# Macaron block on one core: routing found in two parts, the last expert rows loaded over one queue, and a list in a new order

## The chip, the core and the metric

The kernel runs on one core of a Trainium2 chip. The metric is device time in microseconds (us) for one execution. All times below are us unless marked otherwise. The engines are TensorE (PE, with its weight loads shown apart as PEld), VectorE (DVE), ScalarE (ACT), GpSimd (POOL) and SyncE (SP). SP, ACT and POOL can also issue DMAs.

## What is computed

The input is 8 sequences of 512 tokens of width 128, in fp32. Three layers follow each other, each on a normalised copy of the residual stream `x`:

```python
x = x + 0.5 * ffn(layernorm(x), ...)
x = x + attn(layernorm(x), ...)
x = x + 0.5 * ffn(layernorm(x), ...)
```

The same FFN weights serve both times. It is a mixture of experts:

```python
normed = layernorm(x) * ln_gamma + ln_beta
probs = softmax(normed @ router_w.T)            # 8 experts
top_v, top_i = top_k(probs, 2)
gates = softmax(top_v)
comb = sum(one_hot(top_i, 8) * gates[..., None])
out = sum over e of comb[:, e] * swiglu(normed, gate_up_w[e], down_w[e])   # inner width 384
out = out + swiglu(normed, shared_gate_up_w, shared_down_w)                # inner width 128
```

`swiglu` is `silu(gate) * up @ down`. The attention works in windows of 128 tokens and keeps the 32 largest of each row's 128 scores. It adds its own residual and a second normalisation.

## The kernel before, in words

**Blocks and groups.** The 4096 tokens are 8 blocks of 512 (4 windows of 128 each), in two groups: blocks 0 to 3 and 4 to 7. Each FFN runs once for each group. So there are four expert rounds, named (key, group): (0,0), (0,1), (1,0) and (1,1). Attention runs block by block between the rounds of the first FFN and those of the second: blocks 0 to 3 beside round (0,1), blocks 4 to 7 beside round (1,0).

**From logits to sorted rows.** `norm` (L532) normalises a block, writes its rows to DRAM (`rows`), transposes it, and makes the router's logits (`lg`, L563), which DVE copies into `lgs` (L568). `route` (L593) waits for all four blocks of a group. It makes the softmax (L607 to L614, with an exp on ACT at L611), takes the largest and the second largest of 8 (`first`, L620 to L629, twice, with L632 between), sums both choices (`own`, L647), and counts them over the tokens (`csum`, L648 to L653, and two matmuls, `rank`, L664). From these it gets each row's place among the rows sorted by expert. 32 small matmuls (`inv`, L731) invert that order into `src` (L742), the list of rows to gather.

**Expert rounds.** `experts` (L832) handles 39 tiles of 128 sorted rows. POOL gathers rows from DRAM (L846, 32 gathers for a round), PE transposes four of them at a time (`xTp`, L858), ACT applies scale and bias into `xT` (L863). For each tile, `pair` (L875) brings the weights of that tile's expert (`wt`: SP loads them from DRAM at L901, or DVE copies them from SBUF at L899 in the rounds of `COPIED`), then PE makes gate `pg` and up `pu` (L924), ACT the silu (L932), DVE the product (L935), PE the down product `y` (L940). ACT copies `y` to `yb` (L954), and POOL scatters it to `ys` in DRAM (`put`, L962, 39 scatters for a round).

**Back to the tokens.** `fetch_back` (L972) loads each token's two expert rows (`yg`, two loads of 256 KB for a block). `combine` (L990) multiplies them by the gates and adds them to `x` on DVE (L999, four steps for each of the two). For blocks 4 and 6 of the second FFN (`LAST_ON_PE`), `weigh` makes diagonal matrices of the gates, and `combine_on_pe` (L1021) sums on PE: for each window a product of the identity with `x` and two products of a diagonal with `yg`, 12 matmuls in one operation (L1030); ACT copies the sum back to `x` (L1035). `write` (L1137) stores the block. In the last group the first of a block's two loads is issued by SP (L987), the second by ACT (L984), and the blocks come in the order 4, 6, 5, 7.

**What sets the order.** Nothing is issued as it is written. Every operation is recorded with its engine, a cost, what it reads and writes, and a due time (`Plan.op`, L107). `Plan.schedule` (L144) then lets time run: each engine takes, of the operations that could start first, the one with the smallest due time; and a buffer's slot is given when its first user starts. The list that comes out is the program's order on every engine, and each engine works it off in that order. The due times come from constants by hand (`PACE`, `LAG`, `SHARED`, `ROUTE_B`, `FINISH` and so on, L62 to L69). Where this list leaves PE idle for over 0.75, `emit` (L235) puts in matmuls whose result nobody reads (`unread`, L448), so many that they fill the gap but for 0.4. PSUM is planned as seven banks: at most four for `pg` and `pu`, one for `y`, three for everything else (`ps_m`), seven in all.

Of the kernel before, what the change touches and what calls it, by code (L numbers as in the profile page):

```python
# [19 lines left out]
W = 4  # L20
# [25 lines left out]
LAST = 4  # L46
LAST_ON_PE = (4, 6)
# [14 lines left out]
PACE = (1.79, 2.74, 2.54, 0.71)  # L62
LAG, STRETCH, ROUTE_STRETCH = 10.7, -1.72, 3.22
NORM_B, NORM_LAG, NORM_STRETCH = 7.11, 0.69, 1.39
SHARED = ((58.99, 4.72), (33.75, 29.05))
SHARED1 = ((79.31, 10.55), (5.29, 29.83))
ROUTE_B = 39.98
PAIRS, PUTS = 0.2, 10.21
FINISH = 21.26  # L69
# [183 lines left out]
def kernel(  # L253
# [338 lines left out]

    def route(key, g):  # L593
# [6 lines left out]
        def t(tag, shape, dtype=F32):  # L600
            return buf(shape, tag, f"{tag}_{key}_{g}", dtype)

        lgs, alls = r.lgs, [(r.lgs, i) for i in range(GB)]
        mx, sm, m0, m1, i0, th = (t(n, [P, GW, 1]) for n in ("mx", "sm", "m0", "m1", "i0", "th"))
        pr, eq, o0, o1, own = (t(n, full) for n in ("pr", "eq", "o0", "o1", "own"))
        B = 0.29
        dve(B, lambda: ve.tensor_reduce(mx()[:, :, 0], lgs(), AX.X, ALU.max), alls, [mx],  # L607
            after=[(before_[3], 0.0)])
        dve(B, lambda: ve.tensor_tensor(pr(), lgs(), mx().to_broadcast(full), ALU.subtract),
            [*alls, mx], [pr])  # L610
        act(0.29, lambda: nc.scalar.activation(pr(), pr(), AF.Exp), [pr], [pr], table="exp")  # L611
        dve(B, lambda: ve.tensor_reduce(sm()[:, :, 0], pr(), AX.X, ALU.add), [pr], [sm])
        dve(0.25, lambda: ve.reciprocal(sm(), sm()), [sm], [sm])
        dve(B, lambda: ve.tensor_tensor(pr(), pr(), sm().to_broadcast(full), ALU.mult),  # L614
            [pr, sm], [pr])

        dve(B, lambda: ve.scalar_tensor_tensor(pr(), pr(), TINY, pr(), ALU.is_ge, ALU.mult),
            [pr], [pr])

        def first(o, m):  # L620

            dve(B, lambda: ve.tensor_reduce(m()[:, :, 0], pr(), AX.X, ALU.max), [pr], [m])
            dve(B, lambda: ve.tensor_tensor(eq(), pr(), m().to_broadcast(full), ALU.is_equal),
                [pr, m], [eq])
            dve(B, lambda: ve.tensor_tensor(eq(), eq(), rev8.to_broadcast(full), ALU.mult),
                [eq], [eq])
            dve(B, lambda: ve.tensor_reduce(i0()[:, :, 0], eq(), AX.X, ALU.max), [eq], [i0])
            dve(B, lambda: ve.tensor_tensor(
                o(), rev8.to_broadcast(full), i0().to_broadcast(full), ALU.is_equal), [i0], [o])  # L629

        first(o0, m0)
        dve(B, lambda: ve.scalar_tensor_tensor(pr(), o0(), -4.0, pr(), ALU.mult, ALU.add),  # L632
            [o0, pr], [pr])
        first(o1, m1)

        gates = r.gates = t("gates", [P, 2, GW])
        floor, plan.floor = plan.floor, max(plan.floor, plan.ops[-1].due + 30.0)
        dve(0.17, lambda: ve.tensor_tensor(th(), m0(), m1(), ALU.subtract), [m0, m1], [th])
# [8 lines left out]
        dve(B, lambda: ve.tensor_tensor(own(), o0(), o1(), ALU.add), [o0, o1], [own])  # L647
        dve(0.23, lambda: ve.tensor_copy(csum[0][:, PAD:, :], own()), [own], ["cs0"])  # L648
# [18 lines left out]
        pe(0.7, count, [f"cs{i}", own], [rankb])  # L667
# [16 lines left out]
        for k, o in ((0, o0), (1, o1)):  # L684
            dve(B, lambda o=o: ve.tensor_tensor(eq(), o(), at(), ALU.mult), [o, at], [eq])
            dve(B, lambda k=k: ve.tensor_reduce(posf()[:, k, :], eq(), AX.X, ALU.add),
                [eq], [(posf, k)])
# [187 lines left out]
    def pair(r, key, g, t, pace, came, first, upto):  # L875
# [81 lines left out]
        for i in range(a, b):  # L957
            def put(t=c * CH + i, i=i):
                if last_put:
                    nc.gpsimd.memset(apart, 0.0)  # L960
                last_put.append(t)
                ins = nc.gpsimd.indirect_dma_start(  # L962
                    r.ys, bass.IndirectOffsetOnAxis(ap=r.dst()[:, t : t + 1], axis=0),
                    yb()[:, i, :], None,
                ).ins

                tc.declare_no_dep(ins, group=group, reason="rows of other tokens")
                tc.add_to_no_dep_group(group, ins)

            plan.op("POOL", 1.33, put, [(yb, i), r.dst], [(group, c * CH + i)], lat=3.4)  # L970

    def fetch_back(key, b):  # L972
# [9 lines left out]
        for k in range(2):  # L982
            if key and g == NG - 1 and k:
                plan.op("ACT", 0.6, lambda: nc.scalar.dma_start(yg[1](), ys_t[i, 1]),  # L984
                        written, [yg[1]], lat=4.0)
            else:
                load(0.6, yg[k], lambda k=k: ys_t[i, k], written, [yg[k]], lat=4.0)  # L987
        return yg

# [31 lines left out]
    def combine_on_pe(b, yg, diag):  # L1021
# [3 lines left out]
        def both():  # L1025
            for w in range(W):
                for j, (lhsT, rhs) in enumerate(
                    ((ident, xs[b]), (diag[0](), yg[0]()), (diag[1](), yg[1]()))
                ):
                    nc.tensor.matmul(  # L1030
                        sum_()[:, w, :], lhsT if j == 0 else lhsT[:, w, :], rhs[:, w, :],
                        start=j == 0, stop=j == 2)

        pe(2.65, both, [*diag, *yg, xk], [sum_])
# [106 lines left out]
    def blocks(g):  # L1141
        return range(g * GB, (g + 1) * GB)
# [24 lines left out]
    for g in range(NG):  # L1167
# [20 lines left out]
        for b in sorted(blocks(g), key=lambda b: b % 2):  # L1188
# [45 lines left out]
```

## Time and profile before

| | us |
|---|---|
| runs before | 528.71, 529.16, 531.62, 534.18 |
| median of them | 530.39 |
| the profiled execution's own time | 529.42 |
| its span | 527.7 |
| PE busy | 496.7 (94%) |
| PE weight loads busy | 462.7 (88%) |
| DVE busy | 381.3 (72%) |
| POOL busy | 369.8 (70%) |
| ACT busy | 276.8 (52%) |

The profiled execution is one run of the program; its own time holds 1.7 beside the span of the records. "Busy" is the time with an instruction in work, and for PE it includes the filler matmuls (L448: 280 half-passes; an fp32 matmul is two). An fp32 matmul of 128 columns shows as two records that start 0.112 apart. The largest groups are the expert matmuls `pg`, `pu` and `y` (936 records each) and POOL's 156 scatters and 128 gathers of about 1.0 each.

### The profile page before, as it was taken

What the parts mean: (1) busy time and instruction counts of PE and PEld (TensorE: products, weight loads), DVE (VectorE), ACT (ScalarE), POOL (GpSimd) and SP (SyncE); (2) the same over time, 40 slices, a digit from 0 to 9 for tenths busy, and PEclk for the clock granted to TensorE, in tenths of its full rate; (3) what the DMA queues carried; (4) which work ended last, traced back from release to release, by engine and by line L of the source; (5) the groups of instructions that cost most, each with busy time, mean ns of one, the idle gap of its engine ahead of it and who ended that gap; (6) DMA issues with size and microseconds to landing.
All of it is one profiled execution on the core that took longest, in us unless ns stands there. A gap on an engine that the chain in (4) does not pass through costs nothing.

```text
span 527.7 us, 13534 instructions
## 1 busy us (share of the span) xinstructions
PE 496.7 (94%) x4080; PEld 462.7 (88%) x4080; DVE 381.3 (72%) x1440; ACT 276.8 (52%) x588; POOL 369.8 (70%) x481
## 2 busy tenths in 40 slices
PE   3999999999999999999999989999999999999996
PEld 2977899989998989889888888889998999999995
DVE  6589887565349999985598999996479647744413
ACT  4924334333434999976522687997664333333310
POOL 7305888878877786888536886988836778878840
PEclk9979999999999999999999999999999999999998
DMA  7941111111378344556626443545666136311134
GB/s 225 331 166 34 54 46 52 51 51 51 116 261 310 105 147 147 173 147 192 180 95 207 157 137 103 157 133 185 188 200 193 61 96 208 93 46 51 52 119 157
DMA packets 39611, 72.27 MB, mean 137 GB/s; under 512 B 7604, under 2 KB 17848, under 8 KB 39544
## 3 DMA queue, kind: packets, MB, share of 16 engines
q1 hardware_dynamic: 29880, 51.73, 31.1%
q0 software_dynamic: 9088, 18.63, 11.1%
q10 hardware_dynamic: 576, 1.05, 0.5%
q8 instruction: 38, 0.62, 0.5%
q14 instruction: 29, 0.24, 0.1%
HBM read 54.86 MB, written 16.52 MB: 135 GB/s over the span
## 4 chain that ended last, share of the span: by engine, by line
PE 66%; DVE 15%; DMA 6%; POOL 5%; issue 4%; ACT 3%; POOLq 0%; ACTq 0%
PE pg L924 16%; PE y L940 15%; PE pu L924 15%; DVE tk L1088 3%; DVE am L1084 3%; PE ysh L588 2%; DMA wt<-in_expert_gu 2%; PE unread L448 2%; PE pgs L579 2%; DMA xg<-rows,src 2%; PE pus L582 2%; POOL xg L846 2%; PE xTp L858 2%; PE lg L563 2%; DVE sc L1103 2%
## 5 line engine op out<-in xcount | busy, mean ns | idle before, releaser
L962 POOL DMA_INDIRECT ys<-yb,dst x156 | 159.4, 1022 | 55.7 <-issue 25.6
L846 POOL DMA_INDIRECT xg<-rows,src x128 | 128.5, 1004 | 71.1 <-issue 40.1
L924 PE MATMUL pg<-xT,wt 128*128 (+1 forms) x936 | 132.0, 277 | 7.1 <-issue 3.4
L940 PE MATMUL y<-ew,s 128*128 x936 | 129.6, 277 | 2.4 <-DVE s L935 2.1
L924 PE MATMUL pu<-xT,wt 128*128 (+1 forms) x936 | 130.4, 275 | 0.1
L924 PEld LDWEIGHTS pg<-xT,wt 128*128 128x128 f32 x936 | 117.5, 192 | 14.3 <-issue 8.8
L932 ACT ACTIVATE s<-pg 128x384 f32<-128x384 f32 x156 | 75.9, 489 | 99.3 <-PE pg L924 97.2
L940 PEld LDWEIGHTS y<-ew,s 128*128 128x128 f32 x936 | 116.7, 192 | 9.1 <-DVE s L935 3.8
L924 PEld LDWEIGHTS pu<-xT,wt 128*128 128x128 f32 x936 | 117.0, 192 | 0.5 <-DVE s L935 0.3
L935 DVE TENSOR_TENSOR s<-pu,s 128x384 f32<-128x384 f32 x156 | 85.4, 550 | 39.0 <-PE pu L924 27.5
L899 DVE COPY wt<-egu 128x768 f32 x78 | 44.6, 571 | 54.9 <-PE pu L924 53.5
L954 ACT COPY yb<-y 128x512 f32<-128x512 f32 (+1 forms) x60 | 26.1, 436 | 38.4 <-PE y L940 37.8
L999 DVE SCALAR_TENSOR_TENSOR x<-yg,gates,x 128x128 f32<-128x128 f32 x112 | 35.7, 383 | 11.8 <-DMA yg<-ys 11.8
L448 PEld LDWEIGHTS unread<-ident 128*128 128x128 f32 x280 | 33.0, 193 | 2.8 <-issue 2.8
L863 ACT ACTIVATE xT<-xTp,gb 128x512 f32<-128x512 f32 (+2 forms) x34 | 25.3, 754 | 19.3 <-PE xTp L858 19.2
L448 PE MATMUL unread<-ident 128*128 128x128 f32 x280 | 33.9, 276 | 0.0
L499 ACT ACTIVATE n<-x,nb,rstd 128x128 f32<-128x128 f32 x56 | 22.8, 484 | 5.0 <-DVE nb L479 3.9
L1088 DVE MATCH_REPLACE8 tk<-am,tk 128x128 f32<-128x128 f32 x96 | 25.4, 275 | 0.0
L581 ACT ACTIVATE ss<-pgs 128x512 f32<-128x512 f32 x16 | 9.6, 598 | 25.2 <-PE pgs L579 25.2
L858 PE MATMUL xTp<-ident,xg 128*128 128x128 f32 x128 | 20.1, 274 | 2.3 <-DMA xg<-rows,src 2.3
L512 PE MATMUL nTp<-ident,n 128*128 128x128 f32 x64 | 13.1, 350 | 8.7 <-DVE n L489 8.3
L1084 DVE MAX8 am<-tk 128x8 f32<-128x128 f32 x96 | 20.7, 278 | 0.0
(177 smaller groups left out, 700.6 us busy)
## 6 DMA issues: line engine op xcount, KB each, us to landing
wt<-in_expert_gu SPq DMA_DIRECT2D x78, 384.0 KB
yg<-ys SPq DMA_DIRECT2D x28, 256.0 KB
rows<-n SPq DMA_DIRECT2D x16, 256.0 KB
egu<-in_expert_gu SPq DMA_DIRECT2D x8, 384.0 KB
ys<-yb,dst POOLq DMA_INDIRECT x156
x<-in_x SPq DMA_DIRECT2D x8, 256.0 KB
xg<-rows,src POOLq DMA_INDIRECT x128
out_x<-x SPq DMA_DIRECT2D x8, 256.0 KB
```

Of the source, the lines that this page charges most:

```text
L448: plan.idle = lambda: nc.tensor.matmul(unread, ident, ident, start=True, stop=True)
L846: nc.gpsimd.indirect_dma_start(xg()[:, j, :], None, r.rows, bass.IndirectOffsetOnAxis(ap=r.src()[:, t : t + 1], axis=0),)
L858: nc.tensor.transpose(tp()[:, w, :], xg()[:, w, :], ident)
L899: nc.vector.tensor_copy(to, egu[:, bass.ds(row, 2 * FF)])
L924: nc.tensor.matmul(p()[:, f, :], wt()[:, c * NF + f, :], xT[:, bass.ds(offs[1], P)], start=True, stop=True,)
L932: act(0.49, lambda: nc.scalar.activation(s(), pg()[:, 0:NF, :], AF.Silu), [pg], [s], table="silu")
L935: dve(0.56, lambda: nc.vector.tensor_tensor(s(), pu()[:, 0:NF, :], s(), ALU.mult), [pu, s], [s])
L940: nc.tensor.matmul(y()[:, j, :], s()[:, f, :], ew[:, bass.ds(offs[0] + f * H, H)], start=(f == 0), stop=(f == NF - 1),)
L962: ins = nc.gpsimd.indirect_dma_start(r.ys, bass.IndirectOffsetOnAxis(ap=r.dst()[:, t : t + 1], axis=0), yb()[:, i, :], None,).ins
L999: nc.vector.scalar_tensor_tensor(xs[b][:, w, :], yg[k]()[:, w, :], gates()[:, k, q : q + 1], xs[b][:, w, :], ALU.mult, ALU.add,)
L1084: ve.max(m8()[:, w, :], src()[:, w, :])
L1088: ve.match_replace(tk()[:, w, :], m8()[:, w, :], src()[:, w, :], TAKEN)
```

## The change

There are five edits.

1. `route` no longer takes the two experts of all 16 windows of a group in one chain of DVE steps. A new function, `best_two`, does the same steps for a slice of windows, and is called twice: for the first three blocks (`EARLY = 3`, 12 windows) and for the fourth (4 windows). The tiles are the same; the plan counts each tile's two parts apart. The exp on ACT is there twice as well. The gates, and all from `csum` on, stay in one part.
2. In the last group (round (1,1)) all eight loads of expert rows are issued by SP, in a fixed order, with costs of 0.5 and a latency of 2.8 in the plan; its scatters are planned with a latency of 2.4 instead of 3.4.
3. `combine_on_pe` records three operations instead of one: the identity with `x` as one 512-wide matmul, then the four products with the first rows, then the four with the second.
4. The blocks of a group are finished in the order 4, 5, 6, 7 (and 0, 1, 2, 3) instead of the even ones first.
5. The constants of the due times are new, so the whole list comes out in a new order on every engine.

```diff
+EARLY = 3
-PACE = (1.79, 2.74, 2.54, 0.71)
-LAG, STRETCH, ROUTE_STRETCH = 10.7, -1.72, 3.22
-NORM_B, NORM_LAG, NORM_STRETCH = 7.11, 0.69, 1.39
-SHARED = ((58.99, 4.72), (33.75, 29.05))
-SHARED1 = ((79.31, 10.55), (5.29, 29.83))
-ROUTE_B = 39.98
-PAIRS, PUTS = 0.2, 10.21
-FINISH = 21.26
+PACE = (2.51, 2.74, 2.41, 0.71)
+LAG, STRETCH, ROUTE_STRETCH = 13.21, -3.15, 3.38
+NORM_B, NORM_LAG, NORM_STRETCH = 4.21, -0.9, 1.2
+SHARED = ((54.98, 7.11), (47.75, 30.5))
+SHARED1 = ((55.52, 10.55), (7.41, 29.83))
+ROUTE_B = 33.63
+PAIRS, PUTS = 1.02, 20.88
+FINISH = 9.66
...
+    def best_two(r, lgs, part, at, came, mx, sm, m0, m1, i0, th, pr, eq, o0, o1, own):
+        ve, n = nc.vector, at.stop - at.start
+        full = [P, n, NE]
+        B = 0.13 + 0.01 * n
...
+        def do(fn, r, w, us=B, **k):
+            dve(us, fn, [(x, part) for x in r], [(x, part) for x in w], **k)
+
+        dve(B, lambda: ve.tensor_reduce(mx()[:, at, 0], one(lgs), AX.X, ALU.max),
+            came, [(mx, part)], after=[(before_[3], 0.0)])
+        dve(B, lambda: ve.tensor_tensor(one(pr), one(lgs), wide(mx), ALU.subtract),
+            [*came, (mx, part)], [(pr, part)])
+        act(0.29, lambda: nc.scalar.activation(one(pr), one(pr), AF.Exp),
+            [(pr, part)], [(pr, part)], table="exp")
+        do(lambda: ve.tensor_reduce(sm()[:, at, 0], one(pr), AX.X, ALU.add), [pr], [sm])
+        do(lambda: ve.reciprocal(one(sm), one(sm)), [sm], [sm], us=0.2)
+        do(lambda: ve.tensor_tensor(one(pr), one(pr), wide(sm), ALU.mult), [pr, sm], [pr])
+        do(lambda: ve.scalar_tensor_tensor(one(pr), one(pr), TINY, one(pr), ALU.is_ge, ALU.mult),
+           [pr], [pr])
+        rev = rev8[:, 0:1, :].to_broadcast(full)
+        for o, m in ((o0, m0), (o1, m1)):
+            if o is o1:
+                do(lambda: ve.scalar_tensor_tensor(
+                    one(pr), one(o0), -4.0, one(pr), ALU.mult, ALU.add), [o0, pr], [pr])
+            do(lambda m=m: ve.tensor_reduce(m()[:, at, 0], one(pr), AX.X, ALU.max), [pr], [m])
+            do(lambda m=m: ve.tensor_tensor(one(eq), one(pr), wide(m), ALU.is_equal),
+               [pr, m], [eq])
+            do(lambda: ve.tensor_tensor(one(eq), one(eq), rev, ALU.mult), [eq], [eq])
+            do(lambda: ve.tensor_reduce(i0()[:, at, 0], one(eq), AX.X, ALU.max), [eq], [i0])
+            do(lambda o=o: ve.tensor_tensor(one(o), rev, wide(i0), ALU.is_equal), [i0], [o])
+        do(lambda: ve.tensor_tensor(one(own), one(o0), one(o1), ALU.add), [o0, o1], [own])
...
+        B, parts = 0.29, ((0, EARLY), (EARLY, GB))
+        for part, (a, z) in enumerate(parts):
+            best_two(r, lgs, part, slice(a * W, z * W), [(lgs, i) for i in range(a, z)],
+                     mx, sm, m0, m1, i0, th, pr, eq, o0, o1, own)
...
-            plan.op("POOL", 1.33, put, [(yb, i), r.dst], [(group, c * CH + i)], lat=3.4)
+            plan.op("POOL", 1.33, put, [(yb, i), r.dst], [(group, c * CH + i)],
+                    lat=2.4 if (key, g) == (1, NG - 1) else 3.4)
...
-            if key and g == NG - 1 and k:
-                plan.op("ACT", 0.6, lambda: nc.scalar.dma_start(yg[1](), ys_t[i, 1]),
-                        written, [yg[1]], lat=4.0)
-            else:
-                load(0.6, yg[k], lambda k=k: ys_t[i, k], written, [yg[k]], lat=4.0)
+            last = key and g == NG - 1
+            after = [(order_[0], 0.0)] if last else ()
+            o = load(0.5 if last else 0.6, yg[k], lambda k=k: ys_t[i, k], written, [yg[k]],
+                     lat=2.8 if last else 4.0, after=after)
+            if last:
+                order_[0] = o
...
-        def both():
-            for w in range(W):
-                for j, (lhsT, rhs) in enumerate(
-                    ((ident, xs[b]), (diag[0](), yg[0]()), (diag[1](), yg[1]()))
-                ):
-                    nc.tensor.matmul(
-                        sum_()[:, w, :], lhsT if j == 0 else lhsT[:, w, :], rhs[:, w, :],
-                        start=j == 0, stop=j == 2)
-
-        pe(2.65, both, [*diag, *yg, xk], [sum_])
+        pe(0.85, lambda: nc.tensor.matmul(sum_(), ident, xs[b], start=True, stop=False),
+           [xk], [sum_])
+        for k in range(2):
+            def add(k=k):
+                for w in range(W):
+                    nc.tensor.matmul(
+                        sum_()[:, w, :], diag[k]()[:, w, :], yg[k]()[:, w, :],
+                        start=False, stop=k == 1 and w == W - 1)
+
+            pe(0.9, add, [diag[k], yg[k]], [sum_])
...
-        for b in sorted(blocks(g), key=lambda b: b % 2):
+        for b in blocks(g):
```

In the program that comes out, the filler matmuls are 107 instead of 140 (31 instead of 44 after the last `y`, 32 instead of 57 between the logits of block 3 and the first `pg` of round (1,0)). ACT has 30 loads of a function table instead of 24. DVE has 72 more rows of instructions. The identity products of blocks 4 and 6 (`sum_4`, `sum_6`) stand far ahead of the tail: the first among the tiles of round (1,0), the second ahead of the first transposes of round (1,1). The `yg` loads of blocks 4 to 7 for attention stand on SP behind the first three `wt` loads of round (1,0); before, those of blocks 4 and 5 stood ahead of them. All shared-expert work of the second FFN now stands ahead of round (1,1). From the first gather of round (1,1) on, POOL has 73 indirect DMAs instead of 76. On ACT the four DMA issues of the last group are gone; SP issues all eight in the order of the blocks.

## The prediction

> **What bounds the kernel now.** First the page: TensorE (PE) is busy 94% of the span.
>
> ```profile
> span 527.7 us, 13534 instructions
> ## 1 busy us (share of the span) xinstructions
> PE 496.7 (94%) x4080; PEld 462.7 (88%) x4080; DVE 381.3 (72%) x1440; ACT 276.8 (52%) x588; POOL 369.8 (70%) x481
> ```
>
> A busy PE is not all work: the list of groups has 280 half-passes of filler matmuls (`unread`, L448), 140 in the program's list. So I cut the span into seven stages at fixed points of PE's list (first `pg` of expert round (0,0); logits of block 3 in the second FFN; first `pg` of (1,0); logits of block 7; first `pg` of (1,1); last `y`; end) and asked for each stage's engine times. Columns: stretch, its length, PE, PEld, DVE, ACT and POOL busy (instructions), PE clock, DMA share, GB/s.
>
> ```profile
> 0.00:46.91 46.91, 37.24 (x214) 30.32 (x215) 34.41 (x170) 22.66 (x51) 17.09 (x41) 0.93 0.62 206
> 46.91:253.65 206.74, 201.38 (x1679) 188.79 (x1678) 154.34 (x566) 118.13 (x246) 164.73 (x199) 1.00 0.40 126
> 253.65:289.01 35.36, 32.66 (x283) 29.45 (x281) 28.58 (x117) 11.00 (x24) 18.27 (x27) 1.00 0.50 159
> 289.01:382.36 93.35, 88.94 (x723) 82.48 (x721) 81.37 (x366) 74.11 (x160) 77.16 (x84) 1.00 0.49 151
> 382.36:419.59 37.23, 36.19 (x312) 33.10 (x311) 29.40 (x99) 18.84 (x46) 20.75 (x32) 1.00 0.50 158
> 419.59:507.25 87.66, 84.92 (x745) 83.40 (x744) 48.80 (x110) 30.66 (x60) 70.33 (x100) 1.00 0.28 88
> 507.25:527.70 20.45, 15.35 (x138) 15.15 (x136) 4.38 (x16) 1.44 (x3) 1.47 (x3) 0.92 0.49 161
> ```
>
> Then I counted PE's real work in each stage, in the program lists of both kernels, at start-to-start times of this trace: 0.67 for three expert matmuls, 0.86 for a 512-wide matmul, 0.89 for eight 128-wide passes, 0.44 for four transposes. Work before/after, and fillers before/after: stage 1 20.2/20.3, 24/24; 2 195.4/193.6, 5/11; 3 19.0/22.2, 57/32; 4 84.4/90.4, 9/3; 5 35.1/31.3, 0/6; 6 83.3/81.5, 1/0; 7 5.4/3.6, 44/31. Both kernels hold 442.8 us of work; only idle time can go. It lies in stage 1, in stage 3 (35.36 long with 19.0 of work: the second FFN's first routing is exposed) and in stage 7.
>
> The chain of waits shows the two stalls that the change reaches:
>
> ```profile
> 283.85 3.40 DMA xg<-rows,src
> ...
> 435.20 5.50 DMA xg<-rows,src
> ...
> 507.41 9.83 PE unread L448 x88
> 517.24 5.38 PE sum L1030 x48
> ```
>
> In stage 3 the routing ends in `inv` (276.05 to 277.03); then the chain has 2.40 of sequencer time, POOL's gathers, and the fourth gather's landing, 3.40; fillers cover it. The line at 435.20 is the same gather with eight `yg` loads in flight on SP: 5.50. At the end PE does 9.83 of fillers and then the sums. The timeline of the tail (start, length, engine):
>
> ```profile
> 510.24 1.76 SPq L317 DMA_DIRECT2D yg<-ys  x4
> 510.24 1.81 ACTq L984 DMA_DIRECT2D yg<-ys  x4
> 516.83 1.14 DVE L999 SCALAR_TENSOR_TENSOR x<-yg,gates,x 128x128 f32<-128x128 f32 x4 [10.72 <-DMA yg<-ys]
> ...
> 519.08 3.24 DVE L999 SCALAR_TENSOR_TENSOR x<-yg,gates,x 128x128 f32<-128x128 f32 x12 [1.11 <-DMA yg<-ys]
> ```
>
> The trace's semaphore events put block 4's two loads at 513.6 and 513.8, but fillers held PE until 517.24. DVE started at 516.83, when block 5's first landed, and paused until block 7's at 519.06.
>
> **The change part by part.** Own time 529.42, span 527.7; the profiled run is 0.97 under the median 530.39 of the four runs, beside the two quick ones (528.71, 529.16). Sums are against 529.42.
>
> Tail (stage 7). Times from the last `y`'s end (507.42). The last put still lands so that SP issues 2.82 later (510.24). ACT loses four DMA issues (1.81), SP gets eight (3.66 in the row at 431.96, against 1.76). That earlier row is eight loads on one queue, beside POOL's traffic: they landed 2.64, 3.58, 4.87, 5.57, 6.24, 7.20, 7.89 and 8.70 after the first issue. With that: block 5's loads are third and fourth, at 7.7 and 8.4; four DVE steps are 1.14, so block 5 is done at 10.0; block 7's land at 10.7 and 11.5, done 13.0. Block 7's store then stands alone in the queue; block 4's took 2.35 from issue (520.57) to landing (522.92), so 15.4, and the program's end came 1.25 after the last landing: 16.7. Before: 527.71 - 507.42 = 20.3, so -3.6. PE: 31 fillers end at 6.8, block 4's sums at 8.6, block 6's wait for its landings (9.1, 10.0) and end at 10.9, their copy (0.59) at 11.7: not last. If the loads move without POOL at the tail's own 374 GB/s (0.7 each), it is -5.0; if a straggler lands as block 7's did here (9.0 after the issue), -3.0. I take -3.8, near the one-queue row.
>
> The identity step. Two 512-wide matmuls (0.86 each) go from the tail into stages 4 and 5, where PE is the bound: 1.72 is paid there, and counted in the work above. `sum_4` and `sum_6` then hold two of seven PSUM banks through stage 6; that leaves one for `y` and four for `pg`/`pu`, one less when a transpose needs it. No row shows this; the nearest is ACT's copy of a transpose, 0.79, which holds a bank. Bounds 0 to 12 (eight transposes of 1.5 each: 0.44, two handovers, 0.79); I take 0, since a `pg` bank is free again after its silu (0.49), long before its turn two pairs (4.0) later.
>
> Routing in two parts (stage 3). Before, the fourth block's copy is at 254.65, `own` ends at 265.92 and the gathers' source 278.66. A dependent DVE step of 128x128 starts every 0.32 (258.50, 258.82, 259.14); a 128x32 step is 0.19 in the copy's row, so some 0.20: 18 steps give 2.2. The list has the three blocks' last seven steps and two products between them, yet fewer waits for PE: adding its steps up I get 9.8 from the copy to the last `csum` against 13.3, 3.5 less. Middle: -2.9. One more product (0.55) stands in the later chain: +0.5. SP now sends three `wt` loads and then seven `yg` loads, where four `yg` loads went ahead of the routing's end before: the fourth gather lands beside them, 3.40 at best, 5.50 at worst; I take +0.4 of 2.1, as the `wt` loads were beside it already. Stage 3 is as long as this chain: -2.0. The list itself gives nearly that, 25 fillers fewer (-5.6) and 3.2 more work: -2.4. Bounds: -5.0 if no gap is left beside the fillers, 0 if a landing of 5.50 eats it. In stage 1 the four blocks' logits come together, so the split gains nothing; the third block's ACT work moves behind others, and exp runs twice: 0 to +0.8, +0.4.
>
> Exp twice. ACT loads a table for exp and one for silu at each routing:
>
> ```profile
> 255.92 1.28 ACT L611 ACT_TABLE_LOAD   x1
> 257.22 0.31 ACT L611 ACTIVATE pr<-pr 128x128 f32<-128x128 f32 x1
> ...
> 257.70 1.28 ACT L932 ACT_TABLE_LOAD   x1
> ```
>
> The program's list has 30 loads after and 24 before: 6 x 1.28 = 7.7 more of ACT, 2.9 at a time with the exp, in routings (0,1), (1,0) and (1,1). Behind it queue the silus, and PE for their banks: here PE stood 1.22 (258.73 to 259.95), at routing (1,1) 0.32. So 0.3 to 1.2 each, or nothing where PE has other work: +0.5 in stage 2, +0.3 in stage 5; in stage 3 PE waits for the chain anyway.
> The Trainium skill ("ScalarE: Activation LUTs", What ACT_TABLE_LOAD costs) speaks against this: a change of set is a load of about 1283 ns and a drain of about 1380, 2.66 in all. The load agrees, but the silu follows its load at 259.00 at once, so the trace shows no drain; by the page ACT's bill would be an estimated 16 instead of 7.7, and the sum, with three stalls longer by a drain, an estimated 529.3 instead of 525.2.
>
> The list anew. Stage 2: work -1.8, six fillers more at 0.223 = +1.3, tables +0.5: 0.0. Stage 4: work +6.0 (five pairs stand ahead of block 4's transposes, since its loads come late), six fillers fewer -1.3: +4.6, if the attention's gaps stay. Stage 5: work -3.8, fillers +1.3, tables +0.3: -2.2; less work now covers the last routing. Stage 6: work -1.8; the one gather wait of 1.03 goes, but the second chunk's gathers stand behind two puts, six issues of 1.3 and a landing after the first, some 1.6 late: -1.2. Each of stages 2 and 4 may be off by 2.5, stages 5 and 6 by 1.5: the gaps of a new order are not in this trace.
>
> Sum: +0.4 + 0.0 - 2.0 + 4.6 - 2.2 - 1.2 - 3.8 = -4.2, so 525.2.
>
> **The rivals.**
> All idle time that the shorter filler list stands for goes: stages 2 to 6 by work and fillers alone are -0.5 - 2.4 + 4.6 - 2.5 - 1.8 = -2.6, stage 3 gains up to 2.5 more, the tail reaches -5.0: 519.3 to 523; middle 521. For it: the tail's landings are in the trace. Against: in stage 3 idle time was 16.3 where fillers were 12.7, so a list promises more than it gives.
> POOL and the gathers take the gain: both landings go to 5.50 (+1.7 in stage 3, +2.1 in stage 5): 529.0. Also, from the first gather of (1,1) to the last put there are 73 indirect DMAs; before, 76 of them took 98.93 (409.06 to 507.99), 1.32 each, so 95.0 by POOL. PE needs 9.6 to the first `pg` (as 279.42 to 289.01), 81.5 of work, 3.4 of gaps and 0.6: 95.1. POOL is as late as PE, and a stall cannot be made up. With one of the two: 527 to 529. For it: POOL ran without pause there. Against: it had caught up by the end, where it waited for ACT before its last two puts (0.42 and 0.23).
> Slower: the two held PSUM banks. If every transpose of stage 6 waits, 8 x 1.5 = 12: 537.2. It decides from 0.53 for each of the eight, 4.2 in all. For it: no free bank is left. Against: the margin of 4.0 above.
> That the routing does not run early can be told from the lists: in stages 2 to 5 the three blocks' steps do stand ahead; in stage 1 they don't.
>
> **How the numbers follow.** Forecast 0.50 (522 to 528.5), all idle time gone 0.20, POOL and gathers 0.20, banks 0.10. A measurement of this kernel can tell about 1% from no change: 525.1 to 535.7 around 530.39. The forecast lies on that bound, so half of it counts as faster: 0.25 + 0.20 + 0.02 = 0.47; slower is most of the banks' case, 0.08; the rest, 0.45, is within 1%. Stage errors together (the root of the squares of 2.5, 2.5, 2.2, 1.5, 1.5 and 1) are about 4.8; 8 in 10 is 1.3 times that, 6.2: 519.0 to 531.4.
>
> **What would show it.** Tail right: DVE's first `yg` step within 8 of the last `y`, one unbroken filler run of about 6.9, the end 16 to 17.5 after the last `y`. Routing right: `inv` done with no filler ahead of it in stage 3, and a stage of 32 to 34. Wrong: gathers landing over 5 in stages 3 or 5; PE waiting for ACT's `xT` or silu in stage 6; a stage 4 of over 100, which would mean that the late start of block 4 is not made up.

## The result and the profile after

The changed kernel takes 529.73 (median of 52 runs, 526.26 to 534.32), the kernel before 531.13 (78 runs, 526.16 to 534.66); the ratio is 0.9984 with a 95% interval of 0.9972 to 0.9996. So the change gains 0.9 by the ratio (0.2 to 1.5); 525.2 was forecast, 4.2 less than a profiled execution that lay 1.7 under the median of the 78. The range (519.0 to 531.4) held the time. The profiled execution of the changed kernel took 530.32. (Seven experiments below, e9 to e11 and e15 to e18, ran while the kernel before itself took 641.52 to 653.59, two of them on a chip that had given 530.02 earlier; why is open, and their times are set only against the kernel before beside them.) First the page:

```profile
span 528.6 us, 13459 instructions
...
PE 495.7 (94%) x4002; PEld 457.9 (87%) x4002; DVE 382.4 (72%) x1512; ACT 284.4 (54%) x598; POOL 368.0 (70%) x488
```

PE is as busy as before, and between these two profiled executions the span is 0.9 longer. The same seven stages, cut at the same points of PE's list, without stages 2 and 6 (stretch, its length, then PE, PEld, DVE, ACT and POOL busy, PE clock, DMA share, GB/s):

```profile
0.00:50.51 50.51, 39.53 (x221) 33.09 (x222) 36.69 (x192) 23.53 (x52) 17.56 (x42) 1.00 0.58 193
...
256.13:291.87 35.74, 31.53 (x266) 28.34 (x265) 29.43 (x119) 11.77 (x24) 20.32 (x30) 0.98 0.49 159
291.87:388.85 96.98, 95.04 (x751) 86.75 (x751) 83.64 (x398) 80.19 (x172) 77.26 (x85) 0.99 0.53 166
388.85:425.10 36.25, 33.95 (x284) 29.90 (x282) 27.94 (x99) 16.68 (x42) 21.29 (x33) 1.00 0.39 125
...
511.96:528.61 16.65, 10.76 (x95) 10.38 (x93) 4.47 (x16) 1.44 (x3) 1.29 (x3) 0.91 0.61 197
```

Stage 2 is 205.62 long and stage 6, up to the end of the last `y`, 86.86. Against before: +3.6, -1.1, +0.4, +3.6, -1.0, -1.0 and -3.6 (stage 6 before, up to the same point, was 87.82 and stage 7 20.30). So the gain of stage 7 and the price of stage 4 are there, and stages 1 and 3 went the other way. The chain of waits (start, length, what) answers the lines of before:

```profile
284.18 6.11 DMA xg<-rows,src
...
432.33 5.87 DMA xg<-rows,src
...
517.55 5.17 DMA yg<-ys
```

In stage 3 the fourth gather is issued at 284.18, and its landing is 6.11 of the chain, where before it was 3.40; in stage 6 the gather line is 5.87 (before 5.50). At the end the chain goes through the last load of expert rows, no longer through fillers and sums. The timeline of the tail (the last `y` ends at 511.96):

```profile
511.80 7.09 PE L449 MATMUL unread<-ident 128*128 128x128 f32 x62
...
514.78 3.67 SPq L318 DMA_DIRECT2D yg<-ys  x8
...
519.66 2.34 DVE L1023 SCALAR_TENSOR_TENSOR x<-yg,gates,x 128x128 f32<-128x128 f32 x8 [8.99 <-DMA yg<-ys]
...
521.45 2.05 PE L1055 MATMUL sum<-yg,diag 128*128 128x128 f32 x16 [0.78 <-DMA yg<-ys]
```

SP issues 2.82 after the last `y`, as before. One run of fillers lasts 7.1, DVE's first step is 7.7 after the last `y`, and the program ends 16.65 after it. The forecast had 6.9, "within 8" and 16.7.

ACT's two chains of exp in stage 3:

```profile
255.79 1.28 ACT L952 ACT_TABLE_LOAD   x1
257.08 0.87 ACT L952 ACTIVATE s<-pg 128x384 f32<-128x384 f32 x2
257.97 1.28 ACT L613 ACT_TABLE_LOAD   x1
259.27 0.23 ACT L613 ACTIVATE pr<-pr 128x32 f32<-128x32 f32 x1
```

Each exp has its load of 1.28 before and after it; the list of groups has 30 loads, before 24, as the forecast counted. The silu at 257.08 starts the moment its load ends (255.79 + 1.28).

### The profile page after: what moved, and what is told of

Read it like the earlier page. It is cut to its first block, busy times and chain, and to the rows that moved or that the text cites. A ratio compares the mean times of both kernels' runs of the same rounds, so it can differ in the third digit from the quotient of the medians.

```text
span 528.6 us, 13459 instructions
## 1 busy us (share of the span) xinstructions
PE 495.7 (94%) x4002; PEld 457.9 (87%) x4002; DVE 382.4 (72%) x1512; ACT 284.4 (54%) x598; POOL 368.0 (70%) x488
## 4 chain that ended last, share of the span: by engine, by line
PE 59%; DVE 17%; DMA 7%; POOL 7%; ACT 5%; issue 5%; SPq 0%; POOLq 0%; DVEq 0%; ACTq 0%
PE pg L944 15%; PE pu L944 15%; PE y L960 14%; DMA xg<-rows,src 4%; DVE tk L1113 4%; DVE am L1109 3%; POOL xg L866 3%; POOL ys L982 3%; PE lg L564 2%; PE pgs L580 2%; PE ysh L589 2%; PE xTp L878 2%; PE pus L583 1%; DVE s L955 1%; DMA wt<-in_expert_gu 1%
## 5 line engine op out<-in xcount | busy, mean ns | idle before, releaser
L982 POOL DMA_INDIRECT ys<-yb,dst x156 | 157.4, 1009 | 64.2 <-ACT yb L974 30.0
L944 PEld LDWEIGHTS pg<-xT,wt 128*128 128x128 f32 x936 | 118.4, 193 | 13.5 <-issue 9.3
L883 ACT ACTIVATE xT<-xTp,gb 128x512 f32<-128x512 f32 (+2 forms) x34 | 25.2, 752 | 35.2 <-PE xTp L878 35.2
L1023 DVE SCALAR_TENSOR_TENSOR x<-yg,gates,x 128x128 f32<-128x128 f32 x112 | 32.9, 360 | 13.4 <-DMA yg<-ys 13.3
L449 PEld LDWEIGHTS unread<-ident 128*128 128x128 f32 x214 | 25.9, 196 | 1.4 <-issue 1.4
L449 PE MATMUL unread<-ident 128*128 128x128 f32 x214 | 27.1, 279 | 0.0
L564 PEld LDWEIGHTS lg<-rwT,nT 128*128 128x128 f32 x128 | 21.9, 262 | 1.5 <-ACT nT L555 1.5
L878 PEld LDWEIGHTS xTp<-ident,xg 128*128 128x128 f32 x128 | 15.2, 142 | 8.6 <-DMA xg<-rows,src 5.7
L564 PE MATMUL lg<-rwT,nT 128*128 128x8 f32 x128 | 21.8, 301 | 0.8 <-ACT nT L555 0.7
```

Of the source, the lines that this page charges most:

```text
L449: plan.idle = lambda: nc.tensor.matmul(unread, ident, ident, start=True, stop=True)
L564: nc.tensor.matmul(lg()[:, w, 0:NE], nT()[:, w, :], rwT, start=True, stop=True)
L878: nc.tensor.transpose(tp()[:, w, :], xg()[:, w, :], ident)
L944: nc.tensor.matmul(p()[:, f, :], wt()[:, c * NF + f, :], xT[:, bass.ds(offs[1], P)], start=True, stop=True,)
L982: ins = nc.gpsimd.indirect_dma_start(r.ys, bass.IndirectOffsetOnAxis(ap=r.dst()[:, t : t + 1], axis=0), yb()[:, i, :], None,).ins
L1023: nc.vector.scalar_tensor_tensor(xs[b][:, w, :], yg[k]()[:, w, :], gates()[:, k, q : q + 1], xs[b][:, w, :], ALU.mult, ALU.add,)
```

## The experiments

The fixed points of the seven stages are the same in all kernels below. "Before's list" stands for kernels whose list is that of the kernel before up to the stage in question, "after's list" for that of the changed kernel.

### One part of the change alone (e1, e2, e3)

e1 is the kernel before with `fetch_back`, the sum in three steps, the scatters' latency and the block order of the change.

> The kernel before with edits 2, 3 and 4 alone (one SP queue for the last loads, PE's sum in three steps, blocks in the order 4, 5, 6, 7) and the old constants. Theory A (the tail's gain belongs to these edits, and what cost the gain lies in the startup's list): stage 1 stays at 46.9, the last stage falls from 20.45 to 16.8, the whole is 3.0 to 4.0 faster, less what a new order after 290 takes. Rival (the last stage was short only because the new list left 31 fillers instead of 44 there): the last stage stays at 19 to 20.5 and the whole within 1.

Measured: 528.78 (12 runs), ratio 0.9946 (0.9917 to 0.9975), so 2.9 faster. Stages: 46.80, 208.01, 35.53, 93.29, 38.52, 87.74, and 17.80 in the tail, against 20.30. So 2.5 of the tail's 3.65 belongs to these edits; Theory A had 16.8, and the other 1.15 wasn't taken apart. Stage 6, where two PSUM banks are held, is 87.74 against 87.82: no cost of holding them shows.

e2 is the kernel before with `best_two` alone, e3 with the new constants alone.

> The kernel before with edit 1 alone (routing in two parts), old constants. Theory A: the split does not cost the startup anything, since it makes the chain from the last copy of logits to own shorter (6.4 against 7.7): stage 1 46 to 47.5; stage 3 gains as far as its gathers let it, 33.5 to 35.5; the whole -2 to +0.5. Rival B (the split costs the startup, by the second exp and by ten more DVE steps): stage 1 of 49 or more, the whole +2 or more.

> The kernel before with edit 5 alone (the new constants). Theory A (the new constants put the normalisation of blocks 4 to 7 between block 2 and block 3, so block 3's logits come late and PE's counting stands behind 32 slow half-passes): stage 1 of 49.5 to 51, stage 3 as before (35 to 36), last stage 19 to 21, the whole 2 to 5 slower. Rival B: stage 1 of 46.5 to 47.5, the whole within 1.5.

Measured: e2 551.90, ratio 1.0368 (1.0328 to 1.0409); e3 552.61, ratio 1.0413 (1.0369 to 1.0458). Neither theory held for the whole. In e2 stage 4 takes 113.59 (before 93.35) and in e3 stage 3 takes 50.98 (35.36): the planner makes a longer list when one half of the pair is changed without the other, and what is slow in it wasn't taken apart. So the split and the constants can't be tested apart by planning anew, and most experiments below keep a planned list and move a few operations in it. One number of e2 bears on what follows: its stage 3 takes 31.27, 4.1 less than before. No expert row is loaded beside the gathers there (the first `yg` load on SP is issued at 297.24), and the fourth gather lands 2.56 after its issue.

### The startup: PE's own step (e4, e5, e6, e8)

Timeline of PE, startup of the changed kernel: logits of blocks 4 to 7, then `rank` (L683, L684), fillers, `inv`.

```profile
24.10 6.83 PE L564 MATMUL lg<-rwT,nT 128*128 128x8 f32 x32
...
32.63 0.66 PE L683 MATMUL rank<-csum,ones 128*128 128x136 f32 x2
...
41.62 0.54 PE L751 MATMUL inv<-hot,lanes 128*128 128x32 f16 x15
```

DVE's last `csum` step ends at 29.98, but `rank` starts at 32.63, behind 32 half-passes that take 6.83. In the kernel before the same 32 took 4.55, and `rank` started at 29.79:

```profile
23.54 4.55 PE L563 MATMUL lg<-rwT,nT 128*128 128x8 f32 x32 [0.33 <-ACT nT L554]
...
29.79 0.68 PE L664 MATMUL rank<-csum,ones 128*128 128x136 f32 x2
```

The first theories (e3 to e5) put the difference down to the new order, or to what PE did ahead of the logits. By the starts of the half-passes PE has two steps: 0.213 apart (slow) and 0.112 apart (fast). e4 puts 15 fillers at the head of PE's list:

```
         end = IDLE_FROM
+        for _ in range(15):
+            self.idle()
```

> The changed kernel with 15 filler matmuls put at the head of PE's list, where PE waits 8.3 for the first normalised block; the rest of the list is the same. In the changed kernel's trace PE's half-passes start 0.213 apart up to 34.5, and 0.112 apart after. Theory A (the startup is long because PE is slow until it has been busy for about 12 in a row, and counting stands behind the second group's logits): the faster step is reached by 16, the counting starts at 30 to 30.5 instead of 32.6, stage 1 is 47 to 48, the whole 2.5 to 3.5 faster than the changed kernel. Rival C (the gap at 18.8 to 19.8, or the waits for ACT, put PE back to the slow step whatever came before): 0.213 again at 22 to 31, stage 1 of 50 to 51, no gain. Rival B (the split's chain on DVE sets it): counting starts at 30 but inv is no earlier, stage 1 of 49.5 to 50.5.

Measured: `rank` at 29.93, `inv` at 40.12, stage 1 of 48.20, as Theory A had it; but the median is 532.52, ratio 1.0019 (0.9991 to 1.0047), 2.8 above the changed kernel's median; the two intervals just overlap. Windows of e4 (columns as above):

```profile
7.00:11.00 4.00, 3.03 (x15) 1.71 (x14) 3.41 (x23) 2.32 (x7) 3.83 (x6) 0.93 0.96 291
11.00:16.00 5.00, 4.92 (x24) 4.61 (x24) 4.58 (x36) 4.36 (x12) 1.98 (x3) 0.50 0.30 112
16.00:24.00 8.00, 7.43 (x36) 7.03 (x35) 3.19 (x16) 8.00 (x21) 2.60 (x3) 0.50 0.97 321
```

The half-passes went to 0.112 at 7.1, but from 10.5 to 24.1 the granted clock was 0.50, and they were at 0.213 again. The runs with the lowest mean clock (0.967, 0.968) took 534.05 to 535.83, those with the highest (0.977, 0.978) 527.82 to 531.30. Only a quick run (528.18) has a profile, so what the others lost, and that early fillers are the cause, isn't shown.

e5 keeps the planned list and moves three operations in it. In this and the later diffs `behind` and `ahead` put the operations with the later numbers after the one with the first number; here the logits of block 7 (249) and block 4's first shared product (251) go behind `rank` (150), and DVE's copy of those logits (250) behind a step of the counting:

```
+        behind(150, 249, 251)
+        behind(157, 250)
...
-                    for _ in range(int((idle - IDLE_LEFT) / us)):
+                    n = int((idle - IDLE_LEFT) / us)
+                    for _ in range(9 if n == 21 and o.start < 60 else n):
```

> The changed kernel, its list the same but for the startup: PE's counting (rank) stands behind the logits of block 6, ahead of the logits of block 7 and block 4's first shared product, and 9 filler matmuls instead of 21 stand ahead of inv. Theory A (the startup is 3.6 longer because rank stands in PE's queue behind 32 slow half-passes; DVE had the counts' input ready at 29.97, rank began at 32.63): rank begins at 30.0 to 30.5, inv at 39.0 to 39.6, stage 1 is 47.3 to 48.2, and the whole is 2 to 3 faster than the changed kernel (526.5 to 528). Rival (a later step of the startup has no slack either, or the time is given back before the first routing of the second FFN): stage 1 of 49.5 or more, or the whole within 1 of 529.7.

Measured: `rank` at 30.12, but `inv` at 41.30 (its input was there at 39.55), stage 1 of 49.16, median 528.35, ratio 0.9975 (0.9948 to 1.0002): 1.4 under the changed kernel, within what the intervals can't tell. PE was at the slow step from 28.2 to 38.5, and then the 9 fillers ahead of `inv`, from 39.29 on, held it back. Half of Theory A: the place of `rank` is mended, and PE's queue is still the bound.

e8 is the changed kernel once more.

> The changed kernel once more, for its profile. The granted clock of its runs lies in groups (0.991, 0.994, 0.997), with different times. Theory D (a part of the startup's 3.6 is the clock's state in that one profiled run, where PE was at the slow step without a break up to 34.5): in a run with a mean clock of 0.988 to 0.992 PE has a stretch at the fast step between 22 and 34, and stage 1 is 48 to 50. Theory A alone: stage 1 is 50 to 51 whatever the clock.

Measured: 532.09, mean clock 0.992; slow step without a break up to 33.7, and once more for 3.4 from 43.9 on; stage 1 of 51.42. The mean clock doesn't tell the startup's state; Theory D in this form fell. What settled it was e6, whose startup is, instruction for instruction, that of the kernel before:

```profile
23.60 7.00 PE L563 MATMUL lg<-rwT,nT 128*128 128x8 f32 x32
...
32.30 0.66 PE L664 MATMUL rank<-csum,ones 128*128 128x136 f32 x2
```

Here, with before's list, the 32 half-passes take 7.00 and `rank` starts at 32.30, though `csum` was done at 29.64: stage 1 is 49.48, not 46.91. So the same list has two startups, 2.6 apart, by whether PE has a stretch at the fast step between 23 and 31. It had one in 3 of 8 profiles with this order of transposes and in 3 of 11 with the changed order (e4 left out), which tells no difference between them. The forecast's 46.91 was the good case, and the changed kernel's 50.51 was not; slow against slow the change costs 50.8 (mean of 5 profiles, 50.51 to 51.42) - 49.5 (e6 alone) = 1.3. Fast against fast it is 1.3 to 1.4: e4's 48.20 against 46.91 and 46.80 (before and e1), though e4 has the early fillers.

e6 itself is e1 with the identity steps held until the last down product:

```
-           [xk], [sum_])
+           [xk], [sum_], after=[(before_[1], 0.0)])
```

> The kernel before with edits 2, 3 and 4 (as e1), and the two identity steps of PE's sums held back until the last down product, where fillers stood. Theory A (the two steps cost their 1.72 where PE is the bound, and nothing in the tail): 1.3 to 2.0 faster than e1, ratio to before 0.990 to 0.993, last stage 16.5 to 18. Rival (they filled gaps in stages 4 and 5 already): same as e1 within 0.7, ratio 0.9935 to 0.996.

Measured: 528.46, ratio 0.9969 (0.9941 to 0.9997). Stages 4 and 5 are 91.27 and 36.69 (e1: 93.29, 38.52), and the tail is 17.45. Stages 4 and 5 are together 3.9 shorter than in e1, more than the 1.72 of the two steps; the two ratios can't tell the kernels apart.

### The gathers of stage 3 (e7, e10, e13)

e7 is the changed kernel with one 512-byte DMA on SP, which reads the fourth gathered tile (1419), ahead of the seven `yg` loads (from 1773 on):

```
+        behind(1419, 1773, 1774, 1831)
+        i = [o.n for o in order].index(1773)
+        order.insert(i, Op(-1, "SP", 0.3, self.hold, 2.0, None))
```

> The changed kernel with one small DMA more on SP, which reads the fourth gathered tile of round (1,0), ahead of the first seven expert-row loads: these wait until the four gathers have landed. Theory A (the loads on SP beside the gathers take what the split routing gains: the fourth gather's rows were there 6.1 after its issue, against 4.2 before): 4.0 to 4.6 now, the first pg of round (1,0) 1.5 to 2 earlier, stage 3 of 33.8 to 34.4; then block 4's attention starts some 5 later and stage 4 grows by 0 to 5. Rival (three weight loads and the last scatters slow the gathers, not the expert rows): still 5.5 or more, stage 3 unchanged at 35.7.

The fourth gather in the chain of waits, and the window of stage 3:

```profile
284.99 3.16 DMA xg<-rows,src
```

```profile
256.98:289.47 32.49, 30.54 (x267) 27.58 (x265) 25.59 (x104) 11.78 (x24) 18.33 (x28) 1.00 0.42 131
```

Landing 3.16 instead of 6.11, stage 3 of 32.49: the expert rows beside the gathers take the split's gain, and the weight loads, which are still there, don't. (The expectation's 4.2 for the kernel before is 3.40 in its chain of waits.) But stage 4 is 102.25, and the median 532.40, ratio 1.0046 (1.0013 to 1.0080). e13 (and e10, the same kernel) puts that DMA behind block 4's two loads, ahead of 1831:

> As e7, but the two loads of block 4 go at once and only those from block 5 on wait for the four gathers. Theory A (the expert rows beside the gathers slow them, each load by about its 0.7, and stage 4 grew by 5 in e7 because block 4's attention started late): fourth gather's rows 4.2 to 5.2 after its issue (6.1 in the changed kernel, 3.3 in e7), stage 3 of 33.2 to 34.6, stage 4 of 97 to 99, the whole 0.5 to 2 faster than the changed kernel. Rival (all of stage 3's gain comes back in stage 4, since the attention of blocks 4 to 7 is as long as the stage): stages 3 and 4 together as in the changed kernel (132 to 133), the whole within 1.

> The kernel of e10 once more, for the same reason. Theory A: fourth gather's rows 4.2 to 5.2 after its issue, stage 3 of 33.2 to 34.6, stage 4 of 97 to 99, the whole 0.5 to 2 faster than the changed kernel. Rival: stages 3 and 4 together 132 to 133, the whole within 1.

```profile
285.09 4.34 DMA xg<-rows,src
```

Measured in e13: stage 3 33.62, stage 4 100.26, together 133.88; 531.43, ratio 0.9987 (0.9966 to 1.0007). The changed kernel has 132.72 for both stages (131.2 to 133.5 in five profiles of this list), e7 134.74. The rival was right: what stage 3 gains by waiting loads comes back in stage 4. In e10 the ratio was 1.0124 (1.0073 to 1.0175).

Something else lies in these stages that the forecast had no term for. While PE waits for the gathers it has little work, and in the changed kernel's profile the granted clock falls to 0.50 right behind that wait:

```profile
286.50:290.19 3.69, 1.40 (x11) 0.97 (x9) 2.12 (x8) 0.00 (x0) 2.83 (x3) 1.00 0.79 270
290.19:293.61 3.42, 3.28 (x16) 3.29 (x17) 3.04 (x13) 0.99 (x2) 2.21 (x2) 0.50 0.70 214
```

An estimate of its price is at most 1.7, half of 3.42. e12 has the same fall at 292.2, e7 and e13 have one at 298.9 and 298.4, behind waits for DVE. e4, e5 and e8 have the same list there and no such fall, nor have before, e1, e6 and e14. What decides it isn't shown.

### The second routing, stage 5 (e9, e12)

In the changed kernel `csum` of routing (1,1) is done 9.1 after the last copy of logits (12.2 before), but `inv` starts 2.2 after its input is there. e12 (and e9, the same kernel) puts `inv`, `signed`, `src` and four gathers together (2071 to 2136), ahead of a shared product, a `pg` and a `y` (2121, 1737, 1725) and what hangs on them:

```
+        ahead(2071, 2073, 2075, 2077, 2078, 2079, 2133, 2134, 2135, 2136)
+        behind(2136, 2121, 1737, 1725)
```

> The changed kernel with the second routing of the second FFN put ahead in three queues: the four groups of inv stand together on PE, ahead of three products of round (1,0) and a shared one; the copies signed and src stand right behind them on DVE; the first four gathers stand ahead of one put on POOL. Nothing else moves. Theory E (in stage 5 the split's 3.5 are given back because inv stands behind that work on PE, 2.2 after its input was ready, and src stands on DVE behind the other tables): inv at most 0.5 after its input, the first gather 2.5 to 4.5 earlier against the last logits, stage 5 of 32.5 to 34.5 against 36.25, the whole 1.5 to 3 faster than the changed kernel. Rival F (stage 5 is bound by PE's 31 of work and stage 6 by POOL's scatters, so an early gather only lets PE wait later): stage 5 of 34 to 36, stage 6 longer by as much, the whole within 1.

> The kernel of e9 once more, since e9 met a state in which the kernel before took 653 too. Theory E: inv at most 0.5 after its input, the first gather 2.5 to 4.5 earlier against the last logits, stage 5 of 32.5 to 34.5 against 36.25, the whole 1.5 to 3 faster than the changed kernel. Rival F: stage 5 of 34 to 36, stage 6 longer by as much, the whole within 1.

```profile
390.29:428.60 38.31, 35.47 (x300) 31.46 (x298) 28.00 (x99) 16.68 (x42) 23.61 (x34) 1.00 0.42 123
428.60:513.17 84.57, 83.01 (x732) 82.08 (x733) 46.77 (x107) 30.50 (x60) 66.50 (x98) 1.00 0.28 87
```

```profile
409.82 1.95 PE L476 MATMUL unread<-ident 128*128 128x128 f32 x16
411.61 0.95 PE L778 MATMUL inv<-hot,lanes 128*128 128x32 f16 x32
```

Measured in e12: `inv` stands together, but still begins 1.8 after its input. The reason is in the lines above: `emit` counts fillers from the planned start times, and now puts 8 of them (16 half-passes, 1.79) ahead of `inv`. The first gather comes 23.7 after the last logits instead of 26.4; the fourth transpose comes only 13.5 after that, since PE has its other work first. Stage 5 is 38.31 and stage 6 84.57, together 122.88; the changed kernel has 36.25 + 86.86 = 123.11. Median 530.13, ratio 0.9974 (0.9945 to 1.0002). Both theories had stage 5 shorter (at most 34.5, or 36). The two stages together are as in the changed kernel, which is Rival F's mark, but with 1.79 of fillers that the changed kernel doesn't have. So it isn't shown that the routing's place doesn't matter: without these fillers the two stages may be shorter by up to 1.8, an estimate that no run tested. (e9: 1.0126, 1.0066 to 1.0187.)

### A version that beat both in one comparison (e11, e14, e16, e18), and the open question (e15, e17)

e14 is e6 with `rank` behind block 6's logits and 3 fillers instead of 22 between `rank` and `inv`. e11, e16 and e18 are the same kernel.

```
+        behind(131, 230, 232)
+        ahead(138, 231)
...
+                    for _ in range((0 if o.start < 36 else 3) if o.start < 42 else n):
```

> The kernel of e6 (the kernel before, with the tail's edits and the identity steps at the end), and in the startup rank stands behind the logits of block 6 on PE, with 3 filler matmuls instead of 22 between rank and inv. Theory D (with the list of the kernel before, stage 1 was 46.9 where PE reached its fast step and 49.5 where it didn't, since rank and the fillers queue on PE): inv at 39 to 39.7 in either state, stage 1 of 46.5 to 47.5, the median 1 to 2 faster than e6, ratio to before 0.988 to 0.994. Rival (without the fillers PE stays at the slow step into the first expert round): first pg half-passes 0.213 apart, stage 1 or 2 longer by 2 or more, no gain.

> The kernel of e11 once more, for the same reason (there rank began at 29.66 and inv at 38.83 with PE at the slow step, stage 1 was 47.01). Theory D: the same here, the median 1 to 2 faster than e6, ratio to before 0.988 to 0.994. Rival: stage 2 longer by what stage 1 gains, no difference to e6 (0.9969).

```profile
23.62 5.29 PE L591 MATMUL lg<-rwT,nT 128*128 128x8 f32 x24
29.81 0.79 PE L692 MATMUL rank<-csum,ones 128*128 128x136 f32 x2 [0.90 <-DVE csum L680]
...
30.82 1.71 PE L591 MATMUL lg<-rwT,nT 128*128 128x8 f32 x8
...
38.98 0.96 PE L759 MATMUL inv<-hot,lanes 128*128 128x32 f16 x32 [0.66 <-DVE hot L737]
```

Measured: 526.96 (6 runs), ratio 0.9895 (0.9864 to 0.9927), better than both kernels. PE is at the slow step throughout up to 35.6, and yet `rank` starts at 29.81 and `inv` at 38.98: stage 1 is 47.13, and 47.01 to 47.07 in the three other profiles, in one of which PE had its fast stretch. Stage 2 is 208.62, as in e6. In e11, e16 and e18, beside a kernel before of 641.52 to 653.59, the ratios were 1.0043 (0.9965 to 1.0122), 1.0014 (0.997 to 1.0058) and 0.9954 (0.9912 to 0.9996): no gain in two of them, and less than half of it in the third. So the gain rests on e14's 6 runs.

> The kernel of e14 once more, beside e15 on the same chip: ratio to before 0.986 to 0.993 as in e14; stage 1 of 46.8 to 47.4 in either state of PE's step.

> The kernel of e14 once more, beside e17: ratio to before 0.986 to 0.993.

e15 and e17 are the changed kernel with the same startup and the late identity steps, each beside e16 and e18.

> The changed kernel with the startup of e14 (rank behind block 6's logits on PE, 3 filler matmuls instead of 22 between rank and inv) and its two identity steps held back until the last down product. Theory (edits 1 and 5, the split routing and the new order, add nothing once the startup is the same: their gain in stage 3 is lost in the gathers' landing, and stages 4 to 6 are together no shorter): stage 1 of 47 to 48, the last stage 16 to 17, the whole within 1.5 of e14 beside it, and 2.5 to 5 faster than the changed kernel (525 to 527). Rival (the split and the new order are worth 2 or more, hidden so far by the startup): 2 or more faster than e14.

> The kernel of e15 once more, since e15 met the state in which the kernel before takes some 640. Theory (the split and the new order add nothing once the startup is the same): within 1.5 of e18 beside it, 2.5 to 5 faster than the changed kernel. Rival: 2 or more faster than e18.

Measured: 648.93 and 656.26, ratios 1.0159 (1.009 to 1.0227) and 1.0085 (1.0043 to 1.0126); that is 9.1 and 7.5 slower than the kernel beside them. Stage 1 was 48.26 and 48.15 (1.1 to 1.2 longer than beside it), the tail 16.72 and 17.02. There the split and the new order cost some 1.2% to 1.4%; beside a kernel before of some 530 it wasn't measured, and stays open.

## Why the prediction was wrong

| Stage | forecast | before's list | after's list | measured |
|---|---|---|---|---|
| 1, both at the slow step | +0.4 | 49.5 | 50.8 | +1.3 |
| 2 | 0.0 | 208.0 | 206.0 | -2.0 |
| 3 | -2.0 | 35.7 | 35.2 | -0.6 |
| 4 | +4.6 | 92.1 | 97.1 | +5.0 |
| 5 | -2.2 | 36.9 | 36.3 | -0.7 |
| 6 | -1.2 | 87.9 | 86.9 | -1.0 |
| 7 | -3.8 | 20.3 | 16.6 | -3.7 |
| sum | -4.2 | | | -1.7 |

Means over the profiles that have that list: before, e1, e6 and e14 for stages 2 and 3, before, e6 and e14 for 4 to 6; after, e4, e5, e7, e8, e12 and e13 as far as their stage is not edited. The sum, -1.7, lies a little outside the ratio's -0.2 to -1.5: single profiles of one list differ by up to 2 in a stage, and the startups of the many runs were not all slow. The forecast time missed by 4.5 (525.2 against 529.73). Of that, 1.7 is the base: the sum was made against 529.42, an execution with the good startup, and the median of 78 runs is 531.13. The rest is in the terms, and there the misses of stages 1, 3 and 5 (together 3.8) were partly made up by stage 2, which the forecast had at 0.0. That the time lies in the range at all owes something to that luck.

- **Tail**: right in its size and near in each of its marks. The step that mattered was reading the one-queue row of 431.96.
- **Stage 3**, "I take +0.4 of 2.1, as the `wt` loads were beside it already": this step failed. The chain up to the gathers was right: 9.6 from the copy to the last `csum` against 13.3, 3.7 less where 3.5 was forecast; 1.7 of it was left when the first gather was issued, and with 0.6 gained between and behind the gathers the stage without the landing is 2.3 shorter in the two profiled executions (forecast 2.4). Then the landing took 2.7 more (6.11 against 3.40), over the upper bound of 2.1, where +0.4 was taken. The row with eight loads beside the gather (5.50) was the nearest for seven loads, and the forecast took the other end. e7 shows cause and size, and e13 that the gain wasn't kept by holding back fewer loads. The rival "POOL and the gathers" described this half; its other half, a long landing in stage 5, isn't there (the fourth gather is issued at 419.54, and PE transposes its rows from 423.63 to 424.07 without a wait), so its 529.0 is near 529.73 partly by luck.
- **Stage 5**: "work -3.8" counted PE's work and took the gaps as fixed. PE stood 2.3 there: 1.08 for the identity step, which waited for DVE's `x`, 0.64 for a `yb` copy, 0.39 and 0.20. Before, PE stood 1.0 there. e12 moved 2.1 from stage 6 to stage 5 and left their sum as it was, with the fillers said above in it.
- **Stage 1**: the forecast took the startup of one profiled run as the startup. Its own term, +0.4, fits up to the first gather (44.37 against e6's 44.03); the stage is +1.3 with PE's step the same, and the rest, behind the gathers, wasn't taken apart. The state of PE's step, 2.6, was missing in the sum.
- **Stage 2** came out 2.0 better than forecast in the means. In the two profiles it is 1.1, all of it in smaller gaps (PE busy 201.4 in both, 206.74 and 205.62 long). This wasn't taken apart.
- **Stage 4**, the exp tables and the held banks: right. PE has no gap beside the table loads of stage 3 (257.97 and 259.52; its one gap there, 1.20 ahead of 267.11, comes 5 behind them, and the trace names no releaser for it), no silu waited behind its load, and no transpose of stage 6 waited for a bank. The wait for the second chunk's gathers is 0.44 + 1.40 = 1.8 (forecast 1.6).

The Trainium skill ("TensorE: Matmul & The Clock Gate", Part 1) says that TensorE starts at half clock, is released by one busy window of about 3.4, that this window runs freely, and that the moment differs from run to run. The last agrees with these runs: the same list was released at 22.8 (before), 23.4 (e1) or only at 35.6 (e6). The release by one busy window doesn't: in the changed kernel PE's records have no gap from 19.78 to 34.2, and its half-passes stayed 0.213 apart.

## What to carry to other kernels

Before a startup's length goes into a sum, look at the distance between PE's matmul starts in more than one execution; a profile with the fast step and one without it are different baselines. A chain that is made shorter is worth only what its last step leaves: count the transfers that will be in flight beside that last step, and take the price from the row with the nearest number of them. Where a planner makes the list, test a part by moving operations inside the planned list, not by planning again, and put what a chain waits for ahead of slow work and fillers in the same queue.

## What the runs showed of the hardware

- PE's fp32 half-passes start 0.213 or 0.112 apart, those of the logits (128x8) as those of the fillers (128x128). PE falls from the fast to the slow step after 3.4 (at 26.3 before, at 28.2 in e5, at 10.5 in e4), in the kernel before in the middle of the logits. The granted clock shows the slow step as 0.50 only after the first change: up to 34.2 the changed kernel's rows show 1.00 while the starts are 0.213 apart.
- In the changed kernel and in e12 the granted clock fell to 0.50 for 3.4 behind PE's wait for the gathers (290.19 and 292.2); in e4, e5 and e8, with the same list there, it didn't.
- Four gathers of 64 KB landed 3.2 after the fourth's issue with no 256 KB load beside them (e7), 4.3 with two (e13), 6.1 with seven (after).
